# Zero-frequency lane of an FFT attention block: from a matrix row with offsets added by DMA to spread lanes multiplied on GpSimd

## The chip, the cores and the metric

The kernel runs on one core of a Trainium2 chip. The metric is the device time of one launch in microseconds (us); the number given for a kernel is the median of its runs. The engines are called PE (TensorE; PEld is its weight load), DVE (VectorE), ACT (ScalarE), POOL (GpSimd) and SP (SyncE, which here only issues DMAs). Each engine works through its own list of instructions in order.

## What is computed

The input is x and a context, 32 batches of 512 tokens with 512 features. An attention block is followed by a mixture of experts. All is float32. The part that matters:

```python
Q = q @ Wq.T + bq
K = mem @ Wk.T + bk
V = mem @ Wv.T + bv
Qf = jnp.fft.fft(Q, axis=-2)
...
QK = hamilton(Qf * filt, Kf * filt)
QKV = hamilton(QK, Vf * filt)
attended = jnp.fft.ifft(QKV, axis=-2).real.astype(query.dtype)
```

`hamilton` multiplies quaternions: the 512 features are four components of 128, and each of a product's four components is a signed sum of four products. `filt` is one complex number for each frequency. The input of an FFT over the tokens is real, so of 512 frequencies only 257 are computed; frequency 0 and the Nyquist frequency 256 have real values, all others complex ones. A bias adds the same to every token, so after the FFT it touches frequency 0 alone.

After this block x is normalised, each token goes to one of eight experts (top 1, at most 1024 tokens each), and the result is added to x.

## The kernel before

There are two stages. The attention stage runs over the 32 batches and takes the span up to about 2006 us; it also routes the tokens to experts. The experts stage follows. The change touches only the first.

**Work of one batch.** PE turns x and the context to frequencies (`forward`, matmuls of L528, L536 and L541), then projects them (`project`, L557): for each of k, q, v and each half c (0: even frequencies, 1: odd ones) eight matmuls of L573 fill a PSUM buffer of two rows of 512 for each of 128 frequencies, real and imaginary part. There are two such buffers, so a projection can start when the one before the last has been emptied. ACT copies half of it to SBUF (`halves`, L589), and two DVE instructions (`block`, L596) write sums and differences of the two halves to `blk` and so empty the buffer. DVE multiplies the quaternions (`matrix_product`, L645): four products (L676), two sums (L679, L681) and two more (L687, L689), once for q times k and once for that times v, in both halves. `components` (L692) turns the product back to components and writes `y`; PE turns it back to tokens (`inverse`, L732); ACT and DVE form `r` (`sines` L739, `part` L746 and L749, `upper` L752), and DMAs on POOL's queue add the rest and the input (`lower` L759, `add_input` L766 and L271).

**Frequencies 0 and Nyquist.** Both are real, so they share row 0 of half 0: the real part holds frequency 0 and the imaginary part Nyquist. Row 0 must be multiplied as two real numbers and not as a complex one:

- ACT copies the Nyquist row to the tile `ny` (`nyquist`, L581) and then sets it to zero in PSUM (`no_imaginary`, L585). Frequency 0 thus goes the way of all the other rows, with imaginary part 0.
- `nyquist_lanes` (L608) sends `ny` to DRAM (L615) and back (L623), spread over the 128 partitions. POOL copies it into an extra column of `blk` (`spread`, L635 to L637). Because of this column the tiles of half 0 are 129 pairs wide (`L = P + 1`) and DVE's instructions 1032 and 516 wide in place of 1024 and 512.
- The three biases, scaled by `offsets` (L318), lie in DRAM in the form of `blk` (`bias`). After DVE has written row 0 of `blk`, a DMA on POOL's queue adds them to that row (`offset`, L628); DVE's L676 must wait for it. From batch 1 on this happens twice in a batch: for q and k together, later for v.
- `components` sums the extra column to `nyo` (L700, L701); `nyquist_row` (L711) sends it to DRAM (L715) and into the imaginary part of row 0 of `y` (L719).

**Order.** All of the attention stage's instructions are put in order by hand. `Timeline` takes pairs of a planned time and a function (`at`, `steps`), sorts them by time and issues them; `in_order` then keeps this order on each engine. A batch `b` has its origin `o = base[b]`; planned origins are `ROW = 57.5` apart. The planned times only set the order: an instruction runs when those before it on its engine are done and its data is there. On POOL's queue the plan of one origin has, among others, `add_x` (L493, 18.7), two context loads (L271, 19.4), the offsets of q and k (25.7), a context addition (L461, 29.0), the offsets of v (35.6), `spread`, `add_input` (41.0), `scatter` of the routing (four L992, 45.0), two stores of the result (`behind`, L271, 48.5) and the second context addition (L461, 53.0). The context that this last one completes is folded by DVE (`fold_ctx`, L480) at 16.3 of the next origin. The projections k, q and v of half 0 are planned at 8.75, 15.65 and 24.75, their L596 at 18.6, 24.4 and 34.6; those of half 1 at 33.8, 41.15 and 49.5.

## Time and profile before

| what | value |
|---|---|
| median of 3 runs | 3650.66 us (3648.25 to 3651.08) |
| the profiled execution | 3644.01 us, of which its span is 3642.1 us |
| PE busy | 3486.9 us, 96% |
| DVE busy | 2467.8 us, 68% |
| ACT busy | 1524.3 us, 42% |
| POOL busy | 1024.4 us, 28% |
| DMA packets | 273023, of them 74612 under 512 bytes |

Shares of the whole span say little here, because the experts stage (about 2100 to 3642 us) uses PE almost alone. The views used below are the busy times in stretches of the span, the sums of waits (who waited, for whom, how long in total, how often, the longest), and the timeline of single instructions: start, duration, engine, line, operation, out<-in, and in brackets how long the engine was idle before and what ended that. A wait for several things is put down to the one that came last; where the engine named was already done, it was another.

### The profile page before, as it was taken

The numbers are of one execution on the slowest core, as the hardware profiler recorded it, in microseconds if no ns is written. First come the engines' busy times: TensorE is split into PE (matmuls) and PEld (weight loads), VectorE is DVE, ScalarE is ACT, GpSimd is POOL, SyncE is SP. The second block draws the span as 40 slices with busy tenths as digits, with TensorE's granted clock in tenths as the row PEclk, the third lists the DMA queues.
The fourth block names the chain that finished last, engine by engine and source line by source line (L and its number), as shares of the span: only waits on it lengthen the run. The fifth ranks groups of instructions, "written<-read, shape, count | busy, mean of one in ns | idle before, by whom it ended". The sixth has DMA issues, their size and how long they took to land. (4 is left out here: it accounts for less than half of the span.)

```text
span 3642.1 us, 39892 instructions
## 1 busy us (share of the span) xinstructions
PE 3486.9 (96%) x14080; PEld 2414.2 (66%) x14080; DVE 2467.8 (68%) x4494; ACT 1524.3 (42%) x2981; POOL 1024.4 (28%) x946
## 2 busy tenths in 40 slices
PE   8899999999999999999996699999999999999998
PEld 4454555555555554555553588888888888888887
DVE  7888898889888888888897545353444444443532
ACT  5667777767555555555553211112112222111111
POOL 3333434343545343534343211100111111011100
PEclk9999999999999999999998799999999999999999
DMA  6767777677665656666645212130313121111200
GB/s 206 170 168 172 172 169 186 164 184 167 134 145 134 145 133 144 135 146 137 145 99 146 73 35 81 32 99 18 101 35 103 37 80 48 48 63 41 87 1 1
DMA packets 273023, 399.15 MB, mean 110 GB/s; under 512 B 74612, under 2 KB 141044, under 8 KB 272823
## 3 DMA queue, kind: packets, MB, share of 16 engines
q0 software_dynamic: 83088, 189.84, 26.1%
q1 hardware_dynamic: 189586, 206.50, 18.1%
q8 instruction: 111, 1.82, 0.2%
q14 instruction: 88, 0.72, 0.1%
q10 hardware_dynamic: 150, 0.27, 0.0%
HBM read 239.50 MB, written 84.75 MB: 89 GB/s over the span
## 5 line engine op out<-in xcount | busy, mean ns | idle before, releaser
L1233 PE MATMUL r_o<-wo,h 128*128 128x256 f32 x3584 | 781.2, 379 | 0.0
L1233 PE MATMUL r<-xt,wi 128*128 128x256 f32 x3584 | 778.2, 380 | 0.8 <-DVE u L1248 0.8
L1233 PEld LDWEIGHTS r<-xt,wi 128*128 128x128 f32 x3584 | 682.0, 190 | 93.7 <-DVE u L1248 1.1
L1233 PEld LDWEIGHTS r_o<-wo,h 128*128 128x128 f32 x3584 | 677.6, 190 | 90.2
L573 PE MATMUL pp_v<-wv,cf 128*128 128x512 f32 x1024 | 470.0, 603 | 56.5 <-DVE before L947 24.6
L573 PE MATMUL pp_q<-wq,qf 128*128 128x512 f32 x1024 | 457.9, 595 | 2.2 <-DVE blk L596 2.2
L573 PE MATMUL pp_k<-wk,cf 128*128 128x512 f32 x1024 | 458.0, 595 | 0.0
L573 PEld LDWEIGHTS pp_v<-wv,cf 128*128 128x128 f32 x1024 | 189.7, 192 | 308.2 <-issue 229.1
L1385 POOL DMA_INDIRECT out<-o,ids x64 | 106.8, 1668 | 912.5 <-ACT o L1382 803.1
L1411 ACT ACTIVATE h<-h 128x512 f32<-128x512 f32 x256 | 160.0, 629 | 473.7 <-DVE h L1241 469.0
L573 PEld LDWEIGHTS pp_k<-wk,cf 128*128 128x128 f32 x1024 | 187.3, 190 | 225.2 <-issue 201.5
L573 PEld LDWEIGHTS pp_q<-wq,qf 128*128 128x128 f32 x1024 | 189.2, 190 | 220.4 <-issue 208.0
L1346 POOL DMA_INDIRECT g<-tokbuf,ids x64 | 80.4, 1256 | 508.9 <-PE ept L1364 490.5
L676 DVE TENSOR_TENSOR pa<-o,blk 128x1032 f32<-128x1032 f32 (+1 forms) x124 | 152.1, 1227 | 103.8 <-DMA blk<-bias 60.5
L676 DVE TENSOR_TENSOR pa<-blk 128x1024 f32<-128x1024 f32 (+1 forms) x128 | 156.3, 1221 | 87.1 <-DMA blk<-bias 75.5
L1382 ACT ACTIVATE o<-u_o,wgt 128x256 f32<-128x256 f32 x96 | 43.5, 500 | 385.8 <-DVE u_o L1241 385.8
L992 POOL DMA_INDIRECT meta<-entry,slot x128 | 167.3, 1307 | 57.1 <-issue 36.9
L1241 DVE TENSOR_TENSOR h<-r,u 128x512 f32<-128x512 f32 x192 | 129.6, 686 | 72.7 <-PE r L1233 72.6
L1248 DVE TENSOR_TENSOR u_o<-r_o,p_o 128x512 f32<-128x512 f32 x16 | 11.1, 691 | 239.4 <-PE r_o L1233 239.4
L896 ACT ACTIVATE tokT<-pt,beta,gamma 128x512 f32<-128x512 f32 x124 | 96.1, 777 | 177.2 <-PE pt L885 168.7
L271 POOL DMA_INDIRECT out<-r,back x64 | 124.8, 1950 | 126.6 <-ACT cf L555 50.9
L679 DVE TENSOR_TENSOR pa<-pa,pb 128x1024 f32<-128x1024 f32 (+1 forms) x128 | 157.1, 1227 | 2.9
(209 smaller groups left out, 5294.2 us busy)
## 6 DMA issues: line engine op xcount, KB each, us to landing
xs<-in_x SPq DMA_DIRECT2D x32, 1024.0 KB
x<-in_x SPq DMA_DIRECT2D x32, 1024.0 KB
tokbuf<-tok SPq DMA_DIRECT2D x32, 1024.0 KB
wi<-in_wi SPq DMA_DIRECT2D x64, 512.0 KB
wo<-in_wo SPq DMA_DIRECT2D x32, 1024.0 KB
qs<-x POOLq DMA_DIRECT2D x61, 512.0 KB
ctx<-in_ctx SPq DMA_DIRECT2D x32, 512.0 KB
r<-in_x POOLq DMA_DIRECT2D x32, 512.0 KB
```

Of the source, the lines that this page charges most:

```text
L271: ins = nc.gpsimd.indirect_dma_start(out=ap if store else t, out_offset=at_row if store else None, in_=t if store else ap, in_offset=None ...
L573: nc.tensor.matmul(w[b][key][:, ri, :], w[b][f][:, dc, lo : lo + P], wt[n][:, dc, :], start=(dc == 0), stop=(dc == DC - 1),)
L676: tt(out, _bc(left, full), right, ALU.mult)
L679: tt(pa[:, :, 0], pa[:, :, 0], pb[:, :, 1], ALU.subtract)
L896: nc.scalar.activation(to, ps, AF.Identity, bias=o, scale=g)
L992: nc.gpsimd.indirect_dma_start(out=meta[t], out_offset=bass.IndirectOffsetOnAxis(ap=w[b]["slot"][:, t : t + 1], axis=0), in_=entry[:, b, t ...
L1233: nc.tensor.matmul(to[:, m, :], lhs(a, m, i), rhs(b, i), start=(i == 0), stop=(i == k - 1))
L1241: tt(c[i], x, y, ALU.add)
L1346: nc.gpsimd.indirect_dma_start(out=t, out_offset=None, in_=tokbuf, in_offset=bass.IndirectOffsetOnAxis(ap=gid[:, e, c : c + 1], axis=0), b ...
L1382: nc.scalar.activation(o[:, d * N : (d + 1) * N], c[2 * h + d][:, m, :], AF.Copy, scale=wgt[:, e, col : col + 1])
L1385: nc.gpsimd.indirect_dma_start(out=a["out"], out_offset=bass.IndirectOffsetOnAxis(ap=tid[:, e, col : col + 1], axis=0), in_=o, in_offset=None,
L1411: [lambda o=o: nc.scalar.activation(o, o, AF.Gelu) for o in out],
```

## The change

Both real frequencies now take the way that Nyquist alone took, and more of the work with them is done apart from the other rows.

- ACT copies both parts of row 0 to `ny` (`real_rows`, 1x1024) after `halves`; nothing is set to zero. What the main product computes for row 0 is no longer used.
- `real_lanes` takes the place of `nyquist_lanes` and `nyquist_row`: one way out and back for all three of q, k and v with both lanes, then the whole of both quaternion products on POOL (15 instructions on tiles of 128 partitions with 8 to 32 elements each), then one way out and back into both rows of `y`.
- The biases lie in an SBUF tile, spread over partitions, and POOL adds them as the first of those 15 instructions. The offset DMAs and the extra column are gone; all tiles of half 0 have 128 pairs.
- `_constants` doubles one row of the inverse table.
- In the plan the multiply stands at 46.0 of the origin (53.0 in batch 0, 42.5 in the last), and the result's way out at 58.5 (60.0, 48.3). All other planned times stay, but that of `halves` in half 0, which is 1.0 earlier.

```diff
@@ project
-                nc.scalar.copy(w[b]["ny"][:, i, :], w[b][key][0:1, 1, :])
-
-            def no_imaginary():
-                row = w[b][key][0:1, 1, :]
-                nc.scalar.activation(row, row, AF.Copy, scale=0.0)
+                nc.scalar.copy(w[b]["ny"][:, i], w[b][key][0:1])
...
+            at(done + 0.05, halves)
             if c == 0:
-                at(done + 0.05, nyquist)
-                at(done + 0.55, no_imaginary)
-            at(done + (1.05 if c == 0 else 0.05), halves)
+                at(done + 0.55, real_rows)
@@ nyquist_lanes -> real_lanes
-            def offset():
-                nc.gpsimd.dma_start(
-                    w[b]["blk", 0][0:1, lo:hi, :, 0 : 2 * P], bias[lo:hi].unsqueeze(0), accum_op=ALU.add
-                )
...
+            def times(l, r, to, name):
+                m = nyp.tile([P, 4, 2, 2, 2], F32, tag="nymm", name=f"nym_{name}_{b}", bufs=1)
+                for g in range(4):
+                    j, h = divmod(g, 2)
+                    right = r[:, :, :: -1 if h else 1, :: -1 if j else 1]
+                    nc.gpsimd.tensor_tensor(
+                        m[:, g], _bc(l[:, :, h, j : j + 1].unsqueeze(3), [P, 2, 2, 2]), right, ALU.mult
+                    )
+                    yield
+                nc.gpsimd.tensor_tensor(m, m, _bc(signs, [P, 4, 2, 2, 2]), ALU.mult)
+                yield
+                nc.gpsimd.tensor_tensor(m[:, 0:2], m[:, 0:2], m[:, 2:4], ALU.add)
+                yield
+                nc.gpsimd.tensor_tensor(to, m[:, 0], m[:, 1], ALU.add)
+                yield
+
+            def multiply():
+                lane = w[b]["nyi"]
+                nc.gpsimd.tensor_tensor(lane[:, :, 0], lane[:, :, 0], bias, ALU.add)
+                yield
+                yield from times(lane[:, 0], lane[:, 1], lane[:, 0], "qk")
+                w[b]["nyo"] = o = nyp.tile([P, 2, 2, 2], F32, tag="nyo", name=f"nyo_{b}", bufs=1)
+                yield from times(lane[:, 0], lane[:, 2], o.rearrange("p l j h -> p l h j"), "v")
...
             at(t, out)
-            at(t + 2.1, back)
-            at(t_blk, offset)
-            at(t + 4.6, spread)
+            at(t + 3.8, back_in)
+            steps(t_mul, 0.1, multiply())
+            at(t_out, out_again)
+            at(t_out + 2.5, back)
@@ components
-                lane = w[b]["nyo"] = nyp.tile([P, 2, 2], F32, tag="nyo", name=f"nyo_{b}")
-                tt(lane[:, :, 0], o5[:, 0, 0, :, P], o5[:, 0, 1, :, P], ALU.add)
-                tt(lane[:, :, 1], o5[:, 1, 0, :, P], o5[:, 1, 1, :, P], ALU.subtract)
@@ the loop over batches
-                nyquist_lanes(b, 1, 3, o + 18.8, o + 20.7)
-                nyquist_lanes(b, 0, 1, o + 44.8, o + 47.0)
+                real_lanes(b, o + 45.4, o + 53.0, o + 60.0)
...
-                nyquist_lanes(b, 0, 2, o + 23.6, o + 25.7)
-                nyquist_lanes(b, 2, 3, o + 34.4, o + 35.6)
+                real_lanes(b, o + 35.1, *((o + 42.5, o + 48.3) if last else (o + 46.0, o + 58.5)))
...
-            nyquist_row(b, o + pt[2] + 0.7)
```

More of the change, by code (lines that the diff above doesn't have):

```diff
@@ L79, in _constants @@
         inv.append(f.transpose(2, 1, 0) * (0.5 * gain * gain / S))
+        if c == 0:
+            inv[0][0] *= 2.0
     even, odd = fwdq
@@ L222, in attention_and_routing @@
     HS = S // 2
-    L = P + 1
     Q = P // DC
@@ L290, in attention_and_routing @@
         wt = {n: wtp.tile([P, DC, D], F32, name=f"w{n}") for n in "kvq"}
-        bias = dr.tile([3, 4, HS], F32, name="bias", bufs=1)
+        bias = wp.tile([P, 3, 2, 2], F32, name="bias")
+        signs = wp.tile([P, 4, 1, 2, 2], F32, name="signs")
         plain = {}
@@ L318, in offsets @@
         def offsets():
-            plain = prodp.tile([1, 3, D], F32, tag="pb", name="bias_plain")
-            for i, n in enumerate("qkv"):
-                nc.scalar.dma_start(plain[:, i, :], a[f"b{n}"])
+            plain = nyp.tile([P, 3, 4], F32, tag="nym", name="bias_plain", bufs=1)
+            with nc.allow_non_contiguous_dma(reason="one row"):
+                for i, n in enumerate("qkv"):
+                    nc.scalar.dma_start(plain[:, i], a[f"b{n}"].rearrange("o (g f) -> f (o g)", g=4))
             yield 7.5
-            t = prodp.tile([1, 3, 4, HS], F32, tag="pa", name="bias_blocks")
-            for i, n in enumerate("qkv"):
-                by = S * FILTER0 if n == "q" else S / gain
-                src = plain[:, i, :].rearrange("o (j h f) -> o h f j", h=2, j=2)
-                for k, (h, sign) in enumerate(((0, 1), (0, 1), (1, 1), (1, -1))):
-                    nc.gpsimd.tensor_scalar(
-                        t[:, i, k, :].rearrange("o (f j) -> o f j", j=2), src[:, h], sign * by, None, ALU.mult
-                    )
-                    yield 0.5
-            nc.sync.dma_start(bias.rearrange("n k x -> (n k x)").unsqueeze(0), t.rearrange("o n k x -> o (n k x)"))
+            for i, by in enumerate((S * FILTER0, S / gain, S / gain)):
+                nc.gpsimd.tensor_scalar(
+                    bias[:, i], plain[:, i].rearrange("p (j h) -> p h j", j=2), by, None, ALU.mult
+                )
+            nc.gpsimd.memset(signs, 1.0)
+            nc.gpsimd.memset(signs[:, 1:4, 0, 0, 0], -1.0)
+            for g, h, j in ((1, 0, 1), (2, 1, 1), (3, 1, 0)):
+                nc.gpsimd.memset(signs[:, g, 0, h, j : j + 1], -1.0)
         def small_tables():
@@ L576, in mm, with real_rows @@
                     )
-            def nyquist():
+            def real_rows():
                 if "ny" not in w[b]:
-                    w[b]["ny"] = nyp.tile([1, 3, D], F32, tag="ny", name=f"ny_{b}", bufs=1)
-                nc.scalar.copy(w[b]["ny"][:, i, :], w[b][key][0:1, 1, :])
-            def no_imaginary():
-                row = w[b][key][0:1, 1, :]
-                nc.scalar.activation(row, row, AF.Copy, scale=0.0)
+                    w[b]["ny"] = nyp.tile([1, 3, 2, D], F32, tag="ny", name=f"ny_{b}", bufs=1)
+                nc.scalar.copy(w[b]["ny"][:, i], w[b][key][0:1])
             def halves():
@@ L593, in block @@
                     w[b]["blk", c] = blkp.tile(
-                        [P, 3, 4, 2 * (P if c else L)], F32, tag=f"blk{c}", name=f"blk{c}_{b}"
+                        [P, 3, 4, 2 * P], F32, tag=f"blk{c}", name=f"blk{c}_{b}"
                     )
-                tt(blk()[:, part, 0 : 2 * P], w[b][key][:, :, 0:HS], w[b]["xz", n, c], op)
+                tt(blk()[:, part], w[b][key][:, :, 0:HS], w[b]["xz", n, c], op)
             at(t0, mm, 0)
@@ L600, in project, with real_lanes @@
             done = t1 + 3.45
+            at(done + 0.05, halves)
             if c == 0:
-                at(done + 0.05, nyquist)
-                at(done + 0.55, no_imaginary)
-            at(done + (1.05 if c == 0 else 0.05), halves)
+                at(done + 0.55, real_rows)
             at(t_blk, block, slice(0, 4, 3), ALU.subtract)
             at(t_blk + 0.6, block, slice(1, 3), ALU.add)
-        def nyquist_lanes(b, lo, hi, t, t_blk):
-            n = hi - lo
+        def real_lanes(b, t, t_mul, t_out):
@@ L613, in out @@
             def out():
-                w[b]["nyid", lo] = dr.tile([n, D], F32, tag=f"nyid{n}", name=f"nyid_{b}_{lo}")
+                w[b]["nyid"] = dr.tile([6, D], F32, tag="nyid", name=f"nyid_{b}")
                 nc.sync.dma_start(
-                    w[b]["nyid", lo].rearrange("n d -> (n d)").unsqueeze(0),
-                    w[b]["ny"][:, lo:hi, :].rearrange("o n d -> o (n d)"),
-                )
+                    w[b]["nyid"].rearrange("n d -> (n d)").unsqueeze(0),
+                    w[b]["ny"].rearrange("o n l d -> o (n l d)"),
+                )
@@ new lines, in back_in @@
+            def back_in():
+                w[b]["nyi"] = nyp.tile([P, 3, 2, 2, 2], F32, tag="nyi", name=f"nyi_{b}", bufs=1)
+                with nc.allow_non_contiguous_dma(reason="two rows"):
+                    nc.sync.dma_start(
+                        w[b]["nyi"].rearrange("p n l h j -> p (n l) h j"),
+                        w[b]["nyid"].rearrange("n (h f j) -> f n h j", h=2, j=2),
+                    )
+            def times(l, r, to, name):
[5 more added lines that the diff above has]
+                        m[:, g], _bc(l[:, :, h, j : j + 1].unsqueeze(3), [P, 2, 2, 2]), right, ALU.mult
+                    )
+                    yield
[5 more added lines that the diff above has]
+                yield
@@ new lines, in multiply, with out_again @@
+            def multiply():
[5 more added lines that the diff above has]
+                yield from times(lane[:, 0], lane[:, 2], o.rearrange("p l j h -> p l h j"), "v")
+            def out_again():
+                w[b]["nyod"] = dr.tile([P, 8], F32, tag="nyod", name=f"nyod_{b}")
+                nc.sync.dma_start(w[b]["nyod"], w[b]["nyo"].rearrange("p l j h -> p (l j h)"))
@@ L620, in back @@
             def back():
-                w[b]["nyi", lo] = nyp.tile([P, n, 2, 2], F32, tag="nyi", name=f"nyi_{b}_{lo}", padded_shape=[P, 3, 2, 2])
-                with nc.allow_non_contiguous_dma(reason="one row"):
-                    nc.sync.dma_start(
-                        w[b]["nyi", lo], w[b]["nyid", lo].rearrange("n (h f j) -> f n h j", h=2, j=2)
-                    )
-            def offset():
-                nc.gpsimd.dma_start(
-                    w[b]["blk", 0][0:1, lo:hi, :, 0 : 2 * P], bias[lo:hi].unsqueeze(0), accum_op=ALU.add
-                )
@@ L632, in spread @@
-            def spread():
-                lane = w[b]["nyi", lo]
-                b5 = w[b]["blk", 0][:, lo:hi].rearrange("p n (r q) x -> p n r q x", r=2)[:, :, :, :, 2 * P :]
-                nc.gpsimd.tensor_copy(b5[:, :, :, 0, :], lane)
-                nc.gpsimd.tensor_copy(b5[:, :, 0, 1, :], lane[:, :, 0, :])
-                nc.gpsimd.tensor_scalar(b5[:, :, 1, 1, :], lane[:, :, 1, :], -1.0, None, ALU.mult)
+                with nc.allow_non_contiguous_dma(reason="two rows"):
+                    marks["row"] = nc.sync.dma_start(
+                        w[b]["y"][0:1, 0].rearrange("o r (g f) -> o (r g) f", f=P),
+                        w[b]["nyod"].rearrange("f x -> x f").unsqueeze(0),
+                    )
@@ L639, in nyquist_lanes @@
             at(t, out)
-            at(t + 2.1, back)
-            at(t_blk, offset)
-            at(t + 4.6, spread)
+            at(t + 3.8, back_in)
+            steps(t_mul, 0.1, multiply())
+            at(t_out, out_again)
+            at(t_out + 2.5, back)
         def matrix_product(b, c, second):
-            n, name = (P, L)[c == 0], f"{b}_{c}_{int(second)}"
+            n, name = P, f"{b}_{c}_{int(second)}"
             blk = w[b]["blk", c]
@@ L654, in matrix_product @@
             ab = [
-                prodp.tile([P, 16 * L], F32, tag=tag, name=f"{tag}_{name}")[:, 0 : 16 * n].rearrange(
-                    "p (g r x) -> p g r x", g=2, r=2
-                )
+                prodp.tile([P, 2, 2, 4 * n], F32, tag=tag, name=f"{tag}_{name}")
                 for tag in ("pa", "pb")
@@ L682, in matrix_product @@
             yield
-            o = blkp.tile([P, 8 * L], F32, tag="prod", name=f"o_{name}", bufs=2)
-            w[b]["o", c] = o = o[:, 0 : 8 * n].rearrange("p (b x) -> p b x", b=4)
+            w[b]["o", c] = o = blkp.tile([P, 4, 2 * n], F32, tag="prod", name=f"o_{name}", bufs=2)
             o4 = o.rearrange("p (r q) (f j) -> p r (q f) j", r=2, j=2)
@@ L696, in components @@
             o5 = w[b]["o", c].rearrange("p (r q) (f j) -> p r q j f", r=2, j=2)
-            if c == 0:
-                lane = w[b]["nyo"] = nyp.tile([P, 2, 2], F32, tag="nyo", name=f"nyo_{b}")
-                tt(lane[:, :, 0], o5[:, 0, 0, :, P], o5[:, 0, 1, :, P], ALU.add)
-                tt(lane[:, :, 1], o5[:, 1, 0, :, P], o5[:, 1, 1, :, P], ALU.subtract)
-                yield
             y5 = w[b]["y"][:, c].rearrange("p r (j h f) -> p r j h f", j=2, h=2)
-            main = slice(0, P)
-            tt(y5[:, :, :, 0, :], o5[:, :, 0, :, main], o5[:, :, 1, :, main], ALU.add)
+            tt(y5[:, :, :, 0, :], o5[:, :, 0], o5[:, :, 1], ALU.add)
             yield
-            tt(y5[:, 0, :, 1, :], o5[:, 1, 0, :, main], o5[:, 1, 1, :, main], ALU.subtract)
-            tt(y5[:, 1, :, 1, :], o5[:, 0, 1, :, main], o5[:, 0, 0, :, main], ALU.subtract)
+            tt(y5[:, 0, :, 1, :], o5[:, 1, 0], o5[:, 1, 1], ALU.subtract)
+            tt(y5[:, 1, :, 1, :], o5[:, 0, 1], o5[:, 0, 0], ALU.subtract)
             yield
-        def nyquist_row(b, t):
-            def out():
-                w[b]["nyod"] = dr.tile([P, 4], F32, tag="nyod", name=f"nyod_{b}")
-                nc.sync.dma_start(w[b]["nyod"], w[b]["nyo"].rearrange("p j h -> p (j h)"))
-            def back():
-                with nc.allow_non_contiguous_dma(reason="one row"):
-                    marks["row"] = nc.sync.dma_start(
-                        w[b]["y"][0:1, 0, 1, :].rearrange("o (g f) -> o g f", f=P),
-                        w[b]["nyod"].rearrange("f (o g) -> o g f", o=1),
-                    )
-            at(t, out)
-            at(t + 2.1, back)
         def inverse(b, c):
```

## The prediction

> **What bounds the kernel now.** First I read the busy times by stretch. The span has an attention stage to about 2006 us and an experts stage after it; the diff touches only the first. A stretch in the middle, with columns stretch, length, PE, PEld, DVE, ACT, POOL, granted clock, DMA share, GB/s:

> ```profile
> 1201.00:1316.00 115.00, 113.17 (x407) 61.55 (x407) 100.90 (x183) 62.35 (x117) 52.17 (x48) 1.00 0.61 137
> ```

> PE is nearly full at full clock and ACT and POOL are half idle. DVE looks as if it had 14 us to spare, so the next view is who waits for whom, from 166 to 1891 us (in total, times, longest):

> ```profile
> PE pp_v L573 <- DVE before L947: 24.6, 20, 2.2
> PE pp_v L573 <- DVE blk L596: 15.0, 20, 1.5
> ...
> DVE pa L676 <- DMA blk<-bias: 134.3, 42, 5.4
> DVE pa L676 <- POOL blk L637: 50.3, 15, 5.4
> ```

> The eight rows of PE sum to 54.8 us. From the timeline a batch starts (first matmul of L528) every 60.6 us (261.01 to 1836.78 in 26 batches), so 166 to 1891 holds 28.5 batches: PE waits 1.92 us in each. DVE is busy 1515.0 us there (the 15 stretches summed), 53.2 in each batch, and waits 184.6, 6.5 in each. So DVE is taken for 59.7 of 60.6 us, and 6.5 of them go to exactly what the change removes: DVE writes row 0 of `blk`, POOL issues a DMA that adds the offsets, DVE reads it back.

> Is PE's wait the result? The timeline where both meet:

> ```profile
> 1240.67 1.38 POOL L461 DMA_DIRECT2D ctx<-in_ctx  x1
> 1255.09 1.22 DVE L480 TENSOR_TENSOR cs<-ctx 128x1024 f32<-128x1024 f32 x1
> 1259.82 0.68 DVE L596 TENSOR_TENSOR blk<-pp_k,xz_k 128x512 f32<-128x512 f32 x1
> 1260.65 0.67 PE L573 MATMUL pp_v<-wv,cf 128*128 128x512 f32 x1 [1.33 <-ACT tok L857]
> ```

> The batch began at 1232.71. The v projection needs the PSUM buffer that L596 empties: L596 ends at 1260.50, PE goes on at 1260.65. The releaser named (L857, L947 in other batches) only ended near that time. DVE does this L596 at +27.1; its plan says +19.2. It had no idle time since its bias wait at 1222.76, so it is late because of those waits. PE is the bound, and DVE's lateness adds 1.92 us a batch.

> **The change part by part.** *Removed on DVE:* 6.5 us of waits; 12 instructions of 1032 become 1024 wide (1.228 to 1.212 us, about 0.2), four of 516 become 512 (0.04) and two `nyo` sums go (2 x 0.15). DVE needs about 52.7 us. PE's own work is 60.6 - 1.92 = 58.7, so DVE gets 6.0 us of slack. If nothing new is late, the period is 58.7.

> *ACT:* per batch three copies (0.574) and three scalings (0.571) of 1x512 go, 3.4 us; three copies of 1x1024 come. Nearest row: 128x1024 takes 1.06, so 3.2. `halves` moves 1.0 us forward, ahead of the row copy. PSUM is then let go by the later of row copy and L596; the row copy comes out of the plan about 1.7 us after the matmuls, L596 some 5 us after. Cost nothing under that cover; uncovered it is under 1 us.

> *DMAs and SP:* two out-and-back pairs become one, the way back grows from 768 to 1536 packets of 8 bytes, the result's from 512 to 1024 packets of 4. The 516 small ones of the result (L719) landed 2.7 us after issue, so about 4 us, 24 us ahead of the inverse that reads the row. On SP's queue the loads of x and ctx stand behind these waits, as they do today behind the same kind (L615, L715), 20 us ahead of their use. Cost 0 to 0.3 us a batch; I take 0.

> *POOL* is where it is decided. Off: two offset DMAs (0.97 + 0.81) and six small copies. On: 1 + 2 x 7 = 15 tensor_tensor of 8 to 32 elements, queued after the four `meta` scatters and in front of the two `out` stores and the last context addition (L461). In front of DVE's fold (L480) that addition is needed, and the fold stands in front of the L596 for which PE waits. What does one small POOL instruction cost? The trace has them beside an idle DVE (1204.10: 0.19, 0.18, 0.24) and beside a busy one:

> ```profile
> 1217.13 1.22 DVE L681 TENSOR_TENSOR pa<-pa,pb 128x1032 f32<-128x1032 f32 x1
> ...
> 1217.98 0.49 POOL L635 COPY blk<-nyi 128x4 f32<-128x4 f32 x1
> ...
> 1218.27 0.17 DVE L208 SCALAR_TENSOR_TENSOR ex_e<-ex_e,ex_r 128x20 f32<-128x20 f32 x1
> ...
> 1218.34 0.76 POOL L636 COPY blk<-nyi 128x2 f32<-128x2 f32 x1
> 1218.39 0.70 DVE L687 TENSOR_TENSOR o<-pa 128x516 f32<-128x516 f32 x1
> ...
> 1218.50 1.26 POOL L637 TENSOR_SCALAR blk<-nyi 128x2 f32<-128x2 f32 x1
> ...
> 1219.00 0.69 DVE L689 TENSOR_TENSOR o<-pa 128x516 f32<-128x516 f32 x1
> ```

> They end at 1218.47, 1219.10 and 1219.76; DVE's end at 1218.44, 1219.09 and 1219.69. One POOL instruction gets through at each end of a DVE instruction. [...]

> [...] The upper end is one for each end of a 1.15 us DVE instruction: 15 x 1.15 = 17. The stretch beside which they will run is like 1235.14 to 1247.15: 12 ends of two-input instructions and 1.28 us of L596, which reads one input from PSUM and holds nothing. 15 instructions need 10 to 12 us of it; I take T = 10. Their data is there: v's row copy ran at 1210.1, the way out took 3.1 us (L615 at 1210.68, L623 at 1213.78), the longer way back some 6, so 1221; POOL gets there at about 1229.

> Now the chain. Before, the first `r` addition (L766) is issued at 1219.12 and L461 at 1240.67, 21.6 us later. The first can start earlier: it waits for the landing of L759, which follows DVE's `upper`, today late by the 3.61 us wait at 1207.09; with the offset DMA and three copies ahead of it gone too, I take 4.4, of which 1.9 is the shorter period itself: 2.5 us against the next batch. L461's landing is at 1246.73 by its semaphore. After: 1246.7 - 2.5 + 10 = 1254.2. PE's v projection could start at 1259.3 (1260.65 - 1.33), and from L480's start to L596's end DVE needs 5.4 (1255.09 to 1260.50), so the addition may land at 1253.9. PE waits 0.3 us instead of 1.92. **Steady sum:** 28.5 x 1.6 = -46 us.

> *First batches:* PE's waits from 66 to 166 us with a DVE releaser are 1.6, 3.6 and 4.6; less than half follows from bias waits (3.4 and 5.0 there at 126.68 and 175.01): -4. *Setup:* twelve POOL scalings of 0.9 us become three small ones and five fills, while PE waits for the context DMA: 0. *Last batch:* no next batch hides POOL. ACT's copy L739 waits 15.8 us there for the `out` store's landing, and the multiply is queued ahead of that store: +10 - 4.4, less DVE's 1.7 at 1927.07: +4.

> Total -46 against the profiled execution's 3644.0 (span 3642.1 and 1.9 around it): 3598. The runs' median, 3650.66, is 6.7 higher: **3605**.

> **Rivals.** *A, slower: the last context addition becomes the bound.* Place: DVE's L480. Each us of T over 9.7 is a us of PE wait in every batch; at T = 11.6 the new wait equals the old 1.92, and from there the change loses. With T = 14 the wait is 4.3: +2.4 x 28.5 = +68, 3719; with T = 12.5, 3675. For it: chains of dependent instructions miss an end of DVE now and then. Against it: POOL copies without DVE beside them cost 0.2, and DVE, no longer late, has gaps.

> *B, part of the gain: the v wait of half 0 stays.* Of PE's 54.8 us, four rows (L947, L208, two of ACT, 36.5) are at half 0's v projection, 1.28 a batch; the rest, 18.3, is mostly at half 1, 0.64 a batch. If T is 11, or DVE stays late for ACT's copies, only half 1's go: -0.64 x 28.5 = -18, 3632.

> **How the numbers follow.** Likeliest case 0.52: 3585 (T = 5: all 54.8 and the first batches' 9.8 gone, -1.1 at the end) to 3622. B 0.14: to 3648. A 0.28, from 3655 up, half of it above 3685. Less than 3585: 0.04. The range 3585 to 3690 leaves out some 0.17. A measurement of this kernel can tell 0.2% (7.3 us) from no change: faster 0.64, same 0.09, slower 0.27.

> **What would show it.** Right: no `blk<-bias` waits; DVE's rows 1024 wide; the L528 starts 58.7 to 59.2 apart; the 15 POOL instructions within 10 us; L480 just before or just after its landing. Wrong: DVE's largest wait is L480 for `ctx<-in_ctx` and PE's before pp_v is over 2 us (A); or POOL's 15 take over 12.

## The result and the profile after

The changed kernel takes 3632.66 us (median of 12 runs, 3627.66 to 3641.22) beside 3644.49 us for the kernel before on the same chip (12 runs, 3637.43 to 3651.08). The ratio is 0.9965, interval 0.9955 to 0.9974: about 12 us faster, where 45 were forecast (the 3650.66 that the forecast starts from is the median of three of these 12 runs). The profiled spans, 3631.8 and 3642.1 us, differ by 10.3.

First the stretch that opened the prediction, and two like it earlier in the attention stage (columns: stretch, length, PE, PEld, DVE, ACT, POOL busy, granted clock, DMA share, GB/s):

```profile
281.00:396.00 115.00, 110.37 (x391) 60.13 (x390) 106.54 (x220) 81.27 (x173) 59.42 (x60) 0.97 0.74 174
626.00:741.00 115.00, 108.31 (x388) 59.20 (x387) 93.90 (x170) 81.58 (x173) 56.24 (x60) 0.97 0.69 168
1201.00:1316.00 115.00, 113.57 (x410) 62.10 (x409) 103.26 (x196) 62.21 (x112) 64.83 (x64) 1.00 0.64 140
```

Late in the stage PE is a little fuller than before. Early, PE is full for only 108 to 110 of 115 us and the clock is 0.97. Before, the same two early stretches had PE at 111.03 and 111.38 and a clock of 0.99 and 1.00. So the stage has two halves, and they fared differently. The batch starts (first matmul of L528, now L531) say how much (first and second half below mean batches 3 to 14 and 15 to 30; half 0 and half 1 are those of the frequencies):

| from the profiled executions | before | after | difference, us |
|---|---|---|---|
| start of batch 3 | 200.8 | 197.5 | -3.3 |
| batches 3 to 14, mean period | 60.70 | 61.62 | +11.1 in 12 |
| batches 15 to 30, mean period | 60.44 | 59.03 | -22.6 in 16 |
| from the start of batch 31 to the end | 1745.9 | 1750.3 | +4.4 |

The waits from 166 to 1891 us, in total, times and longest: all of PE's, then the largest three of DVE's:

```profile
PE pp_v L576 <- DVE before L943: 37.6, 17, 5.7
PE pp_v L576 <- ACT tok L853: 1.3, 1, 1.3
PE pp_v L576 <- DVE ex_e L211: 1.0, 1, 1.0
```

```profile
DVE y L745 <- ACT y L735: 84.9, 29, 4.9
DVE cs L483 <- issue: 44.9, 14, 4.5
DVE cs L483 <- DMA ctx<-in_ctx: 23.0, 8, 6.8
```

The 184.6 us of DVE waits for `blk<-bias` and its copies are gone. In their place DVE's fold L483 (L480 before) waits, 90.4 us in four rows. The rows name several releasers, but all 25 of these waits in batches 4 to 30 end 0.05 to 0.25 us after the last context addition (L464) has landed, by its semaphore. (The row of L745 grew from 9.7 us; it stays in experiments 1 and 2, where PE hardly waits.) PE's waits fell only from 54.8 to 39.9 us; the longest grew from 2.2 to 5.7. In batches 3 to 14 they rose from 22.0 to 30.2, in batches 15 to 30 they fell from 26.4 to 9.8.

A late multiply on POOL's timeline (batch 26 starts at 1584.8):

```profile
1583.38 1.05 POOL L643 TENSOR_TENSOR nyi<-nyi,bias 128x12 f32<-128x12 f32 x1
1584.50 3.51 POOL L630 TENSOR_TENSOR nym_qk<-nyi 128x8 f32<-128x8 f32 x4
1588.09 1.11 POOL L634 TENSOR_TENSOR nym_qk<-nym_qk,signs 128x32 f32<-128x32 f32 x1
...
1593.00 1.17 POOL L638 TENSOR_TENSOR nyo<-nym_v 128x8 f32<-128x8 f32 x1
...
1600.77 1.37 POOL L464 DMA_DIRECT2D ctx<-in_ctx  x1
```

The 15 instructions take 10.8 us (1583.38 to 1594.17), and the context addition comes out 16 us into the batch. Over batches 3 to 30 the 15 took 8.9 to 11.0 us. T = 10 was right.

And POOL's chain ahead of it, in batch 9 (from 565.0) and then in batch 22 (from 1347.9):

```profile
597.23 0.37 SPq L370 DMA_DIRECT2D xs<-in_x  x1
597.62 0.98 POOL L464 DMA_DIRECT2D ctx<-ctx  x1 [2.97 <-DMA ctx<-in_ctx,back]
597.93 0.37 SPq L869 DMA_DIRECT2D tokbuf<-tok  x1
602.43 1.23 POOL L515 DMA_DIRECT2D qs<-x  x1 [3.83 <-ACT qs L511]
604.86 0.88 POOL L755 DMA_DIRECT2D r<-y  x1 [1.19 <-DVE den L963]
614.49 1.21 POOL L762 DMA_DIRECT2D r<-in_x  x1 [8.75 <-DMA r<-y]
```

```profile
1386.59 0.88 POOL L755 DMA_DIRECT2D r<-y  x1 [1.19 <-DVE den L963]
1392.69 1.21 POOL L762 DMA_DIRECT2D r<-in_x  x1 [5.22 <-DMA r<-y]
```

The bracket is the wait of the addition to `r` for the landing of the `r<-y` transfer: 5.2 us in batch 22, 8.75 in batch 9, where a 1 MB load of x for the statistics (L370) and a store (L869) leave just ahead. Over batches 3 to 14 the addition starts 50.0 us into the batch on average, in batches 15 to 29 at 44.5. Before, it started at 49 to 52 in batches 3 to 13 too, and at 45 to 48 in most later ones. What it waited for there is in the lines of before, first batch 9 (from 565.6), then batch 19 (from 1172.4):

```profile
604.84 0.90 POOL L759 DMA_DIRECT2D r<-y  x1 [1.21 <-DVE den L967]
...
615.05 0.19 POOL L635 COPY blk<-nyi 128x4 f32<-128x4 f32 x1 [4.16 <-DMA nyi<-nyid]
...
615.52 1.27 POOL L766 DMA_DIRECT2D r<-in_x  x1
```

```profile
1219.12 1.88 POOL L766 DMA_DIRECT2D r<-in_x  x1
```

In both the addition comes straight behind the copies of `spread`. By its semaphore `r<-y` had landed 49.0 us into batch 9, just ahead of the copies, and 44.6 into batch 19, 2.1 ahead of the addition. So with the copies gone there were some 2 us to win in batch 19 and less than 1 in batch 9.

### The profile page after: what moved, and what is told of

It is laid out like the page before. It is cut to its first block, busy times and chain, and to the rows that moved or that the text cites. A ratio compares the mean times of both kernels' runs of the same rounds, so it can differ in the third digit from the quotient of the medians.

```text
span 3631.8 us, 39890 instructions
## 1 busy us (share of the span) xinstructions
PE 3484.9 (96%) x14080; PEld 2419.9 (67%) x14080; DVE 2465.1 (68%) x4430; ACT 1513.3 (42%) x2885; POOL 1197.4 (33%) x1166
## 5 line engine op out<-in xcount | busy, mean ns | idle before, releaser
L988 POOL DMA_INDIRECT meta<-entry,slot x128 | 175.0, 1367 | 57.7 <-issue 38.4
L1241 DVE TENSOR_TENSOR u_o<-r_o,p_o 128x512 f32<-128x512 f32 x16 | 11.1, 691 | 239.7 <-PE r_o L1226 239.7
L699 DVE TENSOR_TENSOR pa<-pa,pb 128x1024 f32<-128x1024 f32 x128 | 157.4, 1230 | 2.9
L701 DVE TENSOR_TENSOR pa<-pa,pb 128x1024 f32<-128x1024 f32 x128 | 156.0, 1219 | 0.0
L696 DVE TENSOR_TENSOR pb<-blk 128x1024 f32<-128x1024 f32 x128 | 155.9, 1218 | 0.0
L696 DVE TENSOR_TENSOR pa<-blk 128x1024 f32<-128x1024 f32 x128 | 155.8, 1217 | 0.1
```

Source lines behind the costliest of these rows:

```text
L696: tt(out, _bc(left, full), right, ALU.mult)
L699: tt(pa[:, :, 0], pa[:, :, 0], pb[:, :, 1], ALU.subtract)
L701: tt(pa[:, :, 1], pa[:, :, 1], pb[:, :, 0], ALU.add)
L988: nc.gpsimd.indirect_dma_start(out=meta[t], out_offset=bass.IndirectOffsetOnAxis(ap=w[b]["slot"][:, t : t + 1], axis=0), in_=entry[:, b, t ...
```

## The experiments

The theory after the result: the multiply is as long as forecast, but the start of POOL's chain did not move in batches 3 to 14, because there the landing of `r<-y` sets it and not DVE. The context addition at the end of POOL's queue is then late for L483, L595 and PE. Rivals: the small packets of the two-row way back, GpSimd slowing DVE, and time lost on DVE itself.

**1. The last context addition in front of the multiply.**

```diff
-                at(o + c1, add_ctx, b + 2, 1)
+                at(o + (45.95 if b > 1 else c1), add_ctx, b + 2, 1)
```

> The changed kernel with one line of its plan moved: from batch 2 on the last context addition stands on POOL's queue just before the multiply in place of after it and the two stores. Theory (the multiply delays that addition, the fold on DVE waits for its landing, PE's v projection waits for the fold, and a PE wait of about 4 us or more also brings a stretch at half clock): batches start 58.3 us apart nearly throughout, DVE's wait before the fold is under 1 us, no half clock between 200 and 1900 us; 28 batches then save about 52 us against the changed kernel, near 3580. Rival 1 (the 40,000 additional small DMA packets make the first half slow): batches 4 to 14 stay near 61 to 62 us, only the second half gains, about 10 us. Rival 2 (POOL's reads of SBUF slow DVE): under 5 us.

Measured: 3588.63 us (3583.72 to 3589.2), ratio to before 0.9843 (0.9826 to 0.9859). From 166 to 1891 us PE's and DVE's waits are these, all of them:

```profile
PE back L728 <- DMA y<-nyod: 5.4, 4, 2.5
```

```profile
DVE y L745 <- ACT y L735: 93.5, 30, 4.2
DVE blk L595 <- ACT ny L584: 44.2, 28, 4.3
DVE r L742 <- ACT r L735: 5.3, 2, 3.1
```

The fold waits no more, and the period is 58.27 in batches 15 to 30 and 58.97 in 3 to 14. In batches 3 to 14 `r<-y` still lands 49.4 us into the batch, as in the changed kernel (49.7): the late landing costs next to nothing once the multiply and the two stores no longer stand between it and the context addition. All 15 instructions, their packets and GpSimd's reads are still there, so packets and GpSimd's reads hold PE for no more than the 5.4 us of the row above. The 9 us that miss from the 3580 expected are partly seen: 5.4 us of PE wait, where the multiply, now later, makes the result's row late for the inverse, and one stretch of half clock.

**2. The multiply on DVE.** The 15 `nc.gpsimd.tensor_tensor` become `nc.vector.tensor_tensor`, planned where their data has landed:

```diff
-                real_lanes(b, o + 35.1, *((o + 42.5, o + 48.3) if last else (o + 46.0, o + 58.5)))
+                real_lanes(b, o + 35.1, *((o + 50.5, o + 52.3) if last else (o + 52.3, o + 58.5)))
```

> The changed kernel with the same 15 instructions of the multiply on DVE, planned behind the components of half 0. Theory: POOL's queue is free of the multiply, so the context addition is issued about 10 us earlier; DVE pays 15 x 0.2 = 3 us a batch of its 6 us of slack; batches 58.3 to 58.8 apart, and the last batch also gets back about 4 us of the end: near 3575 to 3585. Rival 1 (small packets): batches 4 to 14 stay near 61 to 62. Rival 3 (DVE has no slack to pay from): PE waits of 1 to 3 us at the v projections come back, 3630 or more.

Measured: 3583.92 us (3582.98 to 3584.35), ratio 0.9834 (0.9817 to 0.985). Groups by shape (busy in total, mean ns of one), first in the changed kernel, then here:

```profile
L630 POOL TENSOR_TENSOR nym_qk<-nyi 128x8 f32<-128x8 f32 x128 | 91.5, 741 | 2.5
L634 POOL TENSOR_TENSOR nym_qk<-nym_qk,signs 128x32 f32<-128x32 f32 x32 | 26.9, 841 | 2.5
```

```profile
L630 DVE TENSOR_TENSOR nym_qk<-nyi 128x8 f32<-128x8 f32 x128 | 12.9, 161 | 1.1
L634 DVE TENSOR_TENSOR nym_qk<-nym_qk,signs 128x32 f32<-128x32 f32 x32 | 6.1, 192 | 1.2
```

The nine groups of the multiply sum to 304.3 us on POOL and 65.0 on DVE, 9.5 and 2.0 in each batch. The same work costs the engine that was called nearly full 2.0 us a batch, and PE waits 2.7 us in all of batches 3 to 30. DVE's time was not the limit; the multiply's place in POOL's queue was.

**3. The kernel before, without the offset DMAs** (`at(t_blk, offset)` is taken out; the result lacks what the biases add to the two rows).

> The kernel before, without the two offset DMAs of a batch; the biases are left out of its result, everything else stays. It shows the removed half of the change alone. Theory (DVE's waits for the offsets made it late, and PE waited for it): DVE's waits before L676 fall from 6.5 to under 2 us a batch, batches 58.5 to 59 apart, 45 to 55 us less than the kernel before, near 3592. If DVE's lateness had another cause, less than 20 us.

Measured: 3607.64 us (3597.53 to 3608.95), ratio 0.9892 (0.9871 to 0.9914): 36 us off by the medians, not 45 to 55. Batches 15 to 30 fell to 58.40 as expected, batches 3 to 14 only to 60.38. DVE's wait did not go; its largest row is now

```profile
DVE pa L675 <- POOL blk L637: 125.7, 53, 5.6
```

The lane copies of the spread, which followed the offset DMA on POOL, are waited for in its place. So half of the expectation failed. In the kernel before, DVE's wait before L676 was 6.6 us a batch for `blk<-bias` and 0.3 for L637 in batches 15 to 30, but 1.8 and 3.8 in batches 3 to 14: there the copies were late already (in batch 9, shown above, they waited for `nyi<-nyid`). PE's waits at half 0's v projection went from 17.4 us to none in batches 15 to 30, and only from 16.8 to 14.5 in batches 3 to 14.

**4 and 5. More loads in the second half.** The changed kernel with two extra 1 MB loads of x in batches 15 to 29; the first run plans the first of them at 29.2 us into the batch, the second run behind the store of `tokbuf`, at 32.3:

```diff
+            def more(b, i):
+                t = xsp.tile([P, TC, D], F32, tag="xs", name=f"more_{b}_{i}")
+                nc.sync.dma_start(t, tok_rows(x_in[b]))
...
+            if 15 <= b < 30:
+                at(o + 29.2, more, b, 0)
+                at(o + 49.8, more, b, 1)
```

> The changed kernel with two additional 1 MB loads of x in each of the batches 15 to 29, at the planned places where batches 1 to 14 load x for the statistics; nobody reads them. Theory (these loads make the DMA of the lower rows, r<-y, land 10 to 12 us after issue in place of 6, and so delay all that is behind it on POOL, the context addition last): batches 15 to 29 look like 4 to 14, 61 to 62 us apart, with PE waits of 1 to 5 us and stretches at half clock, +30 to +45 us against the changed kernel. Rival (the first half is slow for other reasons, such as ACT's statistics or DVE's factors): under +10 us.

> As the run with additional loads in batches 15 to 29, but the first of the two loads is planned behind the store of tokbuf and so issued about 30.5 us after the batch's start, which is near where the loads of batches 3 to 14 fall (about 32, since they wait for their buffer); in the run before it was issued at 26. Theory (it is this place, right ahead of the additions of ctx, qs and r, that makes r<-y land late): r<-y lands 47 to 50 us after the start of a batch in place of 44 to 46, batches 15 to 29 are 61 to 62 us apart, +30 us or more against the changed kernel. Rival (the amount of traffic counts, not its place, or ACT's and DVE's own work in the first half): as the run before, 60.3 us apart.

Measured: 3648.69 us, ratio 1.0014 (1.0004 to 1.0023), and 3643.94 us, ratio 0.9995 (0.9985 to 1.0004). `r<-y` landed 46.5 and 46.9 us into the batch (44.2 without), the periods were 60.31 and 59.95 (59.03 without), and PE waited 23.8 and 19.1 us in batches 15 to 30 (9.8 without). Loads do delay the landing and lengthen the batch, by about half and a third of what was expected; the exact place that run 5 tried made no further difference. Neither run made the first half's order: there the load leaves at 32.2 and the store of `tokbuf` behind it lands at 46.1 (batch 9), while in run 5 the store left first, at 30.1, and landed at 35.2 (batch 22).

**6. The load of the first half moved.** The statistics load that goes out 32 us into batches 1 to 14 is planned at 36.0, its statistics later:

```diff
-        ahead += [(b, *t) for b in range(1, B) for t in ((20.4, 26.2), (39.2, 46.8))]
+        ahead += [(b, *t) for b in range(1, B) for t in ((20.4, 26.2), (47.5, 50.9))]
...
-                at(base[row] + t1 + 3.0, load_stats, b + 1)
+                at(base[row] + (36.0 if row and t1 == 26.2 else t1 + 3.0), load_stats, b + 1)
```

> The changed kernel with the first of the two statistics loads of batches 1 to 14 planned at 36.0 in place of 29.2, behind the way out of the lanes on SP's queue and so after r<-y is issued; the sums and squares that need it move from 39.2 and 46.8 to 47.5 and 50.9. Nothing else changes, all small packets stay. Theory: in batches 3 to 14 r<-y lands at 43 to 46 in place of 49 to 52, the context addition lands at 18 to 22 after the next start, PE's waits fall to 0 to 1.5 us, no half clock there; batches 3 to 14 are 58.3 to 59.8 apart in place of 61.6, about -29 us, 3604. Rival (other causes in the first half): they stay above 61.

Measured: 3624.01 us (3619.28 to 3627.79), ratio 0.9937 (0.9918 to 0.9956), a third of the gain expected. `r<-y` lands at 47.7 in place of 49.7. The move was half a move: in batch 9 the load left at 39.8 and landed at 50.7, beside `r<-y` (39.0 to 48.2) where it had stood in front. One batch of this run (8) also waited 6.6 us, and 10.2 us at half clock went with it.

**7. A version that beats both.** Experiment 2 cost 4 us at the start (batch 3 at 201.5 for 197.5). Here DVE multiplies from batch 3 on, planned as in experiment 2, and GpSimd before, planned as in the changed kernel (`eng` takes the place of `nc.gpsimd` in the multiply):

```diff
+            eng = nc.vector if b > 2 else nc.gpsimd
```

> The multiply on DVE from batch 3 on and on POOL, as in the changed kernel, in batches 0 to 2, where DVE is late with the start of the pipeline. Theory: batch 3 starts at 197.5 us as in the changed kernel in place of 201.5, the rest is as with the multiply on DVE throughout: 4 us less than that, 3580. If DVE's lateness in batches 1 and 2 has another cause: 3584.

Measured: 3577.74 us (3577.42 to 3578.51), ratio 0.9808 (0.9792 to 0.9824), the fastest here. Batch 3 starts at 196.7, and in the stretch of the first table PE is busy all the time:

```profile
1201.00:1316.00 115.00, 115.00 (x408) 62.20 (x407) 108.14 (x229) 63.77 (x114) 45.06 (x34) 1.00 0.69 147
```

**8. The load left out.** What run 6 had left in the way is taken away:

```diff
+        stale = range(6, B, 2)
...
+            if b in stale:
+                w[b]["xs"] = w[b - 1]["xs"]
+                return
```

> The kernel after, but in batches 1 to 13 the 1 MB statistics load that is issued some 32 us into the batch isn't made: batches 6, 8 ... 30 take their statistics from the tile that the load before left, with a sum in place of a sum of squares, so their normalisation is wrong; every other instruction stays. The run with the load moved left it beside the landing of r<-y (issued 39.8, landed 50.7 in batch 9), so it did not take it away. If the queueing behind that load is what holds r<-y in batches 3 to 14: r<-y lands 44 to 46 us into the batch as in batches 15 to 30, the mean period of batches 3 to 14 falls from 61.6 to about 59.0 as there, and no half clock follows, 31 us: about 3602 beside 3633. If DVE's factors or ACT's statistics in that half hold the chain, r<-y is issued late or its landing stays at 48 to 50, the mean stays over 60.5: 3620 or more.

Measured: 3614.46 us (3612.27 to 3617.9), ratio 0.9914 (0.99 to 0.9928). Batch 9 (from 549.9):

```profile
582.84 0.36 SPq L874 DMA_DIRECT2D tokbuf<-tok  x1
...
588.69 0.88 POOL L760 DMA_DIRECT2D r<-y  x1 [1.19 <-DVE den L968]
...
595.13 1.21 POOL L767 DMA_DIRECT2D r<-in_x  x1 [5.55 <-DMA r<-y]
```

The wait of 8.75 is 5.55. What landed when in that batch, in us from its start (issue to landing):

| | changed kernel | load left out |
|---|---|---|
| `xs<-in_x` L370, the load | 32.2 to 38.9 | none |
| `ctx<-ctx` L464, POOL | 32.6 to 42.8 | 31.5 to 36.2 |
| `tokbuf<-tok` L869, SP | 32.9 to 46.1 | 32.9 to 39.5 |
| `qs<-x` L515, POOL | 37.4 to 46.7 | 36.3 to 41.9 |
| `r<-y` L755, POOL | 39.8 to 49.2 | 38.7 to 44.9 |

The load itself is in before `r<-y` leaves. What it puts off are the store and POOL's two transfers ahead of `r<-y`, and POOL's three land in their order. Over batches 3 to 14 the landing is at 45.7 (49.7 with the load; 44.2 in the second half) and the period 59.73 in place of 61.62: 22.7 of the 31 us expected from this half. One stretch of half clock remains, in batch 14. The theory of the load stands for most of the difference, and DVE's and ACT's other work in this half is not its cause. (The 3602 expected is missed by 12 us, 8 of them here. Another 6.3 were lost after the start of batch 31, 1756.6 for 1750.3; why is not shown.) The last 0.7 us between 59.73 and the second half's 59.03 is not settled.

## Why the prediction was right in direction and wrong in size

- *DVE's bias waits go, and it needs about 52.7 us a batch:* right. No such row is left; 103.26 us in the stretch at 1201, that is 1.95 batches, make 53.0 each.
- *PE alone needs 58.7:* a little high, a batch without waits takes 58.27.
- *T = 10:* right, mean 10.1 in the first half and 10.6 in the second. No run shows the T = 5 at the lower end of the range: the shortest in the changed kernel's trace is 7.3 us, in batch 0, and from batch 3 to 30 it is 8.9.
- *Steady period 59.0 with 0.3 us of PE wait:* the sum is right in batches 15 to 30, 59.03, but with some luck: PE waited 0.61, and its own work was shorter. The context addition landed 21.0 us into the batch (forecast 21.5), again as the sum of errors that cancel: the start of the chain gained less than forecast (below), T was longer, and the two `out` stores behind the multiply took 6.1 us where they had taken 7.9. The gain there was 1.41 a batch in place of 1.6.
- *First batches -4, last batch +4:* right, -3.3 and +4.4; ACT's wait for the `out` store in the last batch grew from 15.78 to 19.15 us.
- **The step that failed: "I take 4.4"**, the earlier start of the `r` addition, together with "28.5 x 1.6". Both were read in one place, batches 19 and 20 of the second half, where the addition stood 46.7 us into the batch.

  In that half it moved from 46.9 to 44.5 on average, by 2.4 and not 4.4: `r<-y` left 1.7 us earlier (38.0 for 39.7) and landed only 1.1 earlier (44.2 for 45.3), and the other 1.3 are the copies that no longer stand between the landing and the addition. It could not leave by the whole 3.61 us earlier that DVE no longer waits: `qs<-x` stands ahead of it on POOL's queue and waits for ACT, and in none of these kernels does `r<-y` leave before 37.2 in batches 3 to 30.

  In batches 3 to 14 it moved by about nothing: it had started at about 50 and starts at 50.0, because the transfer, behind what the load puts off, lands at 49 to 50 in most of them however early it leaves (batch 5: left at 37.3, landed at 49.2; before, 48.9 on average). So there the new 10 us fall on the chain whole: the multiply starts at 62.2 (57.4 in the second half), the context addition lands at 23.1 (21.0), and PE waits 30.2 us where 22.0 was the old sum. Against the forecast of 59.0 the 12 batches lost 12 x 2.62 = 31 us, which is nearly all of what misses from the 45.
- *Uncosted:* in batches 4, 6, 11 and 14 PE waits 4.6 to 5.7 us and the clock is half for a time. Their periods beyond 58.27 and beyond the wait sum to 8.6 us, part of those 31.
- *Rival A* named the right place, the last context addition in front of L480, and the right sign for the first half. It put the cause in T, which it had turn at 11.6; T stayed below, and the missing earlier start did what a longer T would have done. *Rival B*'s 3632 is the time measured, and its place is right: all of the 39.9 us of PE's waits that stay are at half 0's v projection (B had 36.5), those at half 1 are gone. Its cause is not: it put the same wait into every batch, for T = 11 or ACT's copies, where 30.2 of the 39.9 lie in batches 3 to 14 (16.8 before) and 9.8 in the others (17.4 before), and part of the time is half clock.

Where the other 33 us are is shown by experiment 1: with all of the change's work in place and the context addition put in front of the multiply, the gain is 55 us. In the changed kernel all but 12 of these are given back through that one queue. With the multiply on DVE the gain is 59 (experiment 2) and 69 (experiment 7).

## What to carry to other kernels

When work is appended to an in-order queue, list what stands behind it and who waits for that, and put the instruction with the nearest due time in front: one line moved here was worth 44 us. A steady stage is costed by the period of all its batches, by halves at least; look for a second regime before you multiply one batch's slack by all of them. An earlier issue need not move a transfer's landing (37.3 and 39.8 us into the batch both landed at 49.2 here): read the landings, not the issues, in a loaded batch too.

## What the runs showed of the hardware

*Half clock after a PE wait.* In the changed kernel the records show half clock for 6.8, 3.4, 6.8 and 3.4 us from 285.3, 411.6, 715.4 and 903.1, each time from the last 0.4 to 2.4 us of a PE wait of over 4.6 us on. Batch 11, PE's row and the clock around it:

```profile
717.78 4.58 PE L576 MATMUL pp_v<-wv,cf 128*128 128x512 f32 x5 [4.92 <-DVE before L943]
```

```profile
715.00:722.00 7.00, 4.22 (x5) 1.85 (x6) 6.84 (x21) 5.04 (x10) 2.96 (x3) 0.53 0.75 207
722.00:740.00 18.00, 18.00 (x55) 8.88 (x54) 12.99 (x21) 11.47 (x23) 4.43 (x5) 0.99 1.03 255
```

*GpSimd beside a busy DVE.* An 8-element multiplication (L630) took 0.19 to 1.27 us on GpSimd and 0.16 on DVE. All 254 of the 480 instructions of the multiply that took over 0.5 us ended within 0.11 us after the end of a DVE instruction; 19 of them had run past an earlier end. Of the shorter ones 85 had an L595, which reads PSUM, beside them from start to end and no other DVE instruction; they took 0.19 to 0.25 us. DVE did not pay: its 1024-element products (L696 in the changed kernel) took 1.22 us with the multiply on GpSimd and on DVE alike. The 15 instructions took 9.5 us a batch on GpSimd and 2.0 on DVE, 4.7 times, these waits included.
